# Text tokens' inner products in four 32-column tiles of TensorE, from each block's diagonal on

## The chip, the cores and the metric

One core of one Trainium2 chip. The metric is the time of one execution on the device in microseconds. Three runs of the kernel before took 433.48, 433.68 and 434.69 us; the median is 433.68 us.

## The reference, cut to what matters

Cross attention with 8 batches, 112 queries of 320 channels, 20 heads of 16 channels, and a context of 375 tokens of 512 channels, of which the last 4 are prompt tokens and the first 371 text tokens.

```python
q, k_t, v_t = heads(x @ W_q), heads(text @ W_k), heads(text @ W_v)
probs_t  = softmax(q . k_t * 16**-0.5)              # 112 x 371 for each batch and head
text_out = probs_t @ v_t
qsem     = l2norm(probs_t @ text)                   # 112 x 512 for each batch and head
sem      = qsem @ l2norm(ip).T                      # against the 4 prompt tokens
probs_ip = softmax(q . k_ip * scale + 0.5 * sem) * spatial_mask
out      = (text_out + probs_ip @ v_ip) @ W_out + b_out + x
```

The norm of `probs_t @ text` is the square root of p^T G p, where G = text text^T are the text tokens' inner products (371 x 371, symmetric). The kernel therefore never forms `qsem`: it computes G once for each batch, and from G the norms of all 20 heads.

## The kernel before

Each batch goes through 5 groups of 4 heads; a group is a step, and there are 40 steps.

*The Gram matrix.* `gram(b)` computes G in three chunks c0, c1, c2 of 128 token rows, each in a PSUM bank of its own named `ps_g`. A chunk's matmuls take 128 tokens of the transposed context as the stationary operand and the tokens from the chunk's start to the end, prompts included, as the moving one: 375, 247 and 119 columns, over four channel blocks `e`. Each float32 matmul is two hardware passes, so a Gram is 24 loads of weights and 24 passes. Only the upper triangle by chunks is made; `doubled` evicts a chunk with one ScalarE instruction that multiplies by 2 (line 443) and then has GpSimd multiply the diagonal chunk by the mask `half` (line 444), which halves the 32 x 32 blocks on the diagonal, so that the half triangle stands for the whole G. `ug` is the SBUF tile that receives this; one buffer serves all batches. Batch 0's Gram is made by `first_gram` in another order, and calls `doubled` too.

*From the Gram to the products.* `gram_to_groups` copies `ug` by DMA, four DMAs for each block of 32 partitions, to the tile `u` of the batch, where every 32-partition group holds the same tokens for another head. The values (line 526, evicted at line 533 to `vext`) are written to DRAM by `values_to_dram`, read back by `values_to_groups` into `vr` and put behind the Gram's columns in `u` by `placed` on GpSimd. `product` (line 683) multiplies the transposed probabilities of one head, 32 tokens at a time, with the matching 32 rows of `u`, from the diagonal on: 12 products j for each head, 392 columns wide for j = 0 and 32 narrower each time, 40 for the last. The four heads of a group lie on the four 32-row groups of TensorE and write to four banks.

*The order.* The instructions of TensorE, VectorE and SyncE stand in the order in which they are written, and after a prologue those of ScalarE and GpSimd as well. `pair(n)` writes the products of two steps, with the scores (line 632) and probabilities (lines 645 to 658) of the steps two ahead between them; where it passes from one step to the next it writes

```python
for there, here in ((HIGH, LOW), (LOW, HIGH)):
    product(*two, 0, there)
    for j in ends:
        product(b, g, j, here)
```

`behind(n)` writes the projections of the coming batches behind each pair: queries, keys, Gram (`gr`), values, and pieces of the last batch's `finish` (`f`). For an odd batch the three chunks of the Gram are written with other pieces between them, the third behind a piece of `finish` whose ScalarE work is a square root with a table load on either side (lines 801 and 802):

```python
gr(nb); tr(0); gr(nb)
if n: f(b - 1)
gr(nb)
...
v(nb)
```

For an even batch (`gr(nb + 1, 3)`) all three follow each other. Batch 1's Gram is followed by the projections of the prompts (lines 271 and 288), for which GpSimd spreads the weights `wip` (lines 123 and 124).

*The banks.* PSUM has four banks with the tag "qd" and two each with "sc" and "mm"; each tag hands its banks out in turn. `turn` says which tag the next projections take. For odd batches c0, c1 and c2 take three "qd" banks and the values' first chunk an "mm" bank; for even batches c0 takes "qd" and c1 and c2 take "mm". The four products of the next step take the four "qd" banks, and a product waits until its bank has been evicted. Two of the coming scores take "mm" banks.

Of the kernel before, what the change touches and what calls it, by code (L numbers as in the profile page):

```python
# [8 lines left out]
F32 = mybir.dt.float32  # L9
AF = mybir.ActivationFunctionType  # L10
ALU = mybir.AluOpType
# [9 lines left out]
def kernel(  # L21
# [29 lines left out]
    RG = 32  # L51
# [11 lines left out]
    QN = P // RG  # L63
    WC = [UW - c * P for c in range(NT)]
    GCOL = [sum(WC[:c]) for c in range(NT + 1)]
    GW = GCOL[NT]
    UCOL = QN * GW
    assert (H, D, NC, NT, P) == (20, 16, 3, 3, 128) and RG == 2 * D


    groups = [[i * HC + 2 * a + r for a in range(GROUP)] for i in range(2) for r in range(2)]
    groups.append([2 * HC + a for a in range(GROUP)])

    const = ctx.enter_context(tc.tile_pool(name="const", bufs=1))
# [94 lines left out]
    make_identity(nc, ident)  # L169
    nc.gpsimd.memset(wq_sb[REST:, FULL, :], 0.0)  # L170

    half = const.tile([P, P], F32, tag="half", name="half")
    nc.gpsimd.memset(half, 1.0)
    for q in range(QN):
        nc.gpsimd.memset(half[q * RG : (q + 1) * RG, q * RG : (q + 1) * RG], 0.5)

    hmask = const.tile([P, HC], F32, tag="hmask", name="hmask")
    nc.vector.tensor_reduce(
# [10 lines left out]
    ug = const.tile([P, GCOL[NT]], F32, tag="ug", name="ug")  # L189
# [17 lines left out]
    k3 = const.tile([P, NT, GROUP, 2, D], F32, tag="k3", name="k3")  # L207

    def more_constants():
        nc.gpsimd.memset(k3[:, :, :, 1, :], 0.0)  # L210
        nc.gpsimd.memset(wo_sb[REST:, FULL, :], 0.0)
        for at in attn_ring:
            nc.gpsimd.memset(at[:, C:], 0.0)
# [130 lines left out]
    st = {}  # L344
# [93 lines left out]
    def doubled(ps, c):  # L438

        t0 = c * P  # L440
        k = min(P, TT - t0)
        g = ug[:, GCOL[c] : GCOL[c] + T - t0]
        nc.scalar.mul(g, ps[:, : T - t0], 2.0)  # L443
        nc.gpsimd.tensor_tensor(g[:, :k], g[:, :k], half[:, :k], ALU.mult)  # L444

    def gram(b):

        ctxT = st[b]["ctxT"]

        for c in range(NT):  # L450
            t0 = c * P
            ps = bank(f"ps_g_{b}_{c}")
            for e in range(NE):
                nc.tensor.matmul(  # L454
                    ps[:, : T - t0],
                    ctxT[:, e, t0 : t0 + P],
                    ctxT[:, e, t0:T],
                    start=(e == 0),
                    stop=(e == NE - 1),
                )  # L460
            doubled(ps, c)
            yield

    def gram_to_groups(b, blocks):
# [74 lines left out]
            yield  # L539

    def values_to_dram(b, eng, c0=0, c1=NT):
        eng.dma_start(
            st[b]["vd"][c0 * P : c1 * P].rearrange("(c p) x -> p c x", p=P),
            st[b]["vext"][:, c0:c1, :C],
        )

    def values_to_groups(b):
        s = st[b]
# [128 lines left out]
    def product(b, g, j, heads):  # L677
        s = st[b]
        xT = s["xT", g]
        banks = s["qd", g]  # L680
        c, q = j // QN, j % QN
        for a in heads:
            nc.tensor.matmul(  # L683
                banks[a][:S, j * RG : UW],
                xT[a * RG : (a + 1) * RG, j, :S],
                region(b, c)[a * RG : (a + 1) * RG, q, q * RG :],
                start=(j == 0),
                stop=(j == BLK - 1),
            )
# [395 lines left out]
    def gr(b, pieces=1):  # L1085
        run(("g", b), lambda: gram(b), pieces)
# [192 lines left out]
    for n in range(0, len(steps) - NG, 2):  # L1279
# [4 lines left out]
        b, g = steps[n]  # L1284
# [16 lines left out]
    b = B - 1  # L1301
# [12 lines left out]
    for g in range(NG):  # L1314
# [20 lines left out]
        if g < NG - 1:  # L1335

            n = GROUP - 1 if g <= LEAD else 1
# [89 lines left out]
```

## Time and profile before

| | us |
|---|---|
| median of three runs | 433.68 |
| the profiled execution | 434.62 |
| its span, first to last instruction | 432.9 |
| PE busy | 423.2 (98%) |
| DVE busy | 328.5 (76%) |
| ACT busy | 190.7 (44%) |
| POOL busy | 112.1 (26%) |

PE stands for TensorE's matmuls, PEld for its weight loads, DVE for VectorE, ACT for ScalarE, POOL for GpSimd, SP for SyncE, whose queue issues most DMAs. A group's row gives the line, the engine, the operation, the tiles it writes and reads, the shape and the count; then the busy time in us, the mean duration of one in ns, and the idle time of the engine just before, with what ended it. A shape such as 32*112 is rows by columns of the stationary operand. A timeline row gives the start in us, the length in us of a merged run of instructions, and their count. The granted clock of TensorE was 0.995 of full speed over the span.

### The profile page before, as it was taken

How to read it: one execution, taken by the hardware profiler on the slowest of the kernel's cores; microseconds unless marked ns; L12 is line 12 of the kernel's file. 1: busy time of each engine (PE TensorE's matmuls, PEld its weight loads, DVE VectorE, ACT ScalarE, POOL GpSimd, SP SyncE). 2: the span in 40 equal slices, each digit the busy share in tenths (PEclk: the TensorE clock that was granted, in tenths of full speed). 3: DMA queues.
4: the chain of work that ended last, by engine and by line, in shares of the span. 5: the costliest groups of instructions: out<-in, count | busy, mean ns of one | idle time of the engine just before them, and what ended most of it. 6: DMA issues, size and time to landing. Idle time of an engine off the chain costs nothing. (4 is left out here: it accounts for less than half of the span.)

```text
span 432.9 us, 12985 instructions
## 1 busy us (share of the span) xinstructions
PE 423.2 (98%) x5024; PEld 323.8 (75%) x5024; DVE 328.5 (76%) x687; ACT 190.7 (44%) x649; POOL 112.1 (26%) x270
## 2 busy tenths in 40 slices
PE   8999999999999999999999999999999999999986
PEld 8756677778686887778686887778776888776783
DVE  4045467797899897796889898787888897778884
ACT  2264123334553454333643464233633563346793
POOL 4302200012151234012142126002133226026440
PEclk9999899999999999999999999999999999999999
DMA  8669946487554566576744466575755436663300
GB/s 243 171 173 248 213 112 154 143 192 155 148 142 123 157 160 150 152 177 138 181 134 124 127 171 159 144 187 134 173 160 145 111 101 166 175 157 100 101 4 27
DMA packets 57931, 64.21 MB, mean 148 GB/s; under 512 B 18368, under 2 KB 52024, under 8 KB 57870
## 3 DMA queue, kind: packets, MB, share of 16 engines
q1 hardware_dynamic: 57304, 62.66, 57.2%
q8 instruction: 40, 0.66, 0.7%
q10 hardware_dynamic: 566, 0.72, 0.5%
q14 instruction: 21, 0.17, 0.1%
HBM read 18.67 MB, written 5.32 MB: 55 GB/s over the span
## 5 line engine op out<-in xcount | busy, mean ns | idle before, releaser
L683 PE MATMUL ps_qd<-u,xgT 32*112 32x232 f32 (+11 forms) x3840 | 215.4, 352 | 1.9 <-POOL u L599 1.9
L683 PEld LDWEIGHTS ps_qd<-u,xgT 32*112 32x112 f32 x3840 | 180.0, 172 | 36.5 <-issue 8.1
L672 DVE STREAM_TRANSPOSE xgT<-xg 128x768 f32<-128x768 f32 (+1 forms) x63 | 121.2, 1951 | 9.2 <-DMA xg<-p 9.1
L649 ACT ACTIVATE p<-ps_s,nmx 112x371 f32<-112x371 f32 x160 | 85.8, 586 | 52.5 <-DVE nmx L645 48.5
L743 DVE CUSTOM_DVE_ANT_0 junk<-ps_qd,p 112x371 f32<-112x371 f32 x148 | 80.2, 542 | 31.5 <-ACT pvs L710 11.4
L645 DVE TENSOR_REDUCE nmx<-ps_s 112x1 f32<-112x371 f32 x160 | 77.3, 537 | 28.0 <-PE ps_s L632 26.0
L599 POOL COPY u<-vr 128x64 f32<-128x64 f32 x120 | 26.7, 237 | 192.9 <-PE ps_qd L683 116.4
L526 PE MATMUL ps_v<-wv_sb,ctxT 128*128 128x384 f32 (+1 forms) x192 | 63.5, 477 | 0.3 <-ACT kT L499 0.3
L632 PE MATMUL ps_s<-kT,qm 32*112 32x375 f32 (+1 forms) x320 | 61.9, 487 | 1.0 <-ACT shared L728 0.7
L526 PEld LDWEIGHTS ps_v<-wv_sb,ctxT 128*128 128x128 f32 x192 | 35.4, 190 | 20.7 <-ACT kT L499 1.2
L710 ACT COPY pvs<-ps_qd 112x21 f32<-112x21 f32 x150 | 21.4, 200 | 62.2 <-DVE ss L743 61.0
L492 PE MATMUL ps_k<-ctxT,wk_sb 128*128 128x371 f32 x136 | 45.8, 481 | 0.0
L454 PE MATMUL ps_g<-ctxT 128*128 128x375 f32 (+2 forms) x168 | 36.8, 375 | 0.0
L454 PEld LDWEIGHTS ps_g<-ctxT 128*128 128x128 f32 x168 | 28.3, 191 | 8.7
L492 PEld LDWEIGHTS ps_k<-ctxT,wk_sb 128*128 128x128 f32 x136 | 24.6, 190 | 13.4 <-issue 0.5
L632 PEld LDWEIGHTS ps_s<-kT,qm 32*112 32x112 f32 x320 | 27.9, 171 | 6.9 <-ACT shared L728 1.3
L533 ACT COPY vext<-ps_v 128x384 f32<-128x384 f32 (+1 forms) x24 | 11.2, 466 | 37.1 <-PE ps_v L526 37.0
L651 ACT COPY ipl<-ps_s 112x4 f32<-112x4 f32 x140 | 24.2, 173 | 0.0
L443 ACT ACTIVATE ug<-ps_g 128x375 f32<-128x375 f32 (+2 forms) x24 | 9.0, 377 | 29.4 <-PE ps_g L454 20.5
L499 ACT COPY kT<-ps_k 128x371 f32<-128x371 f32 x17 | 8.0, 469 | 30.8 <-PE ps_k L492 30.8
L336 DVE TENSOR_SCALAR qm<-ps_q,emask 128x224 f32<-128x224 f32 (+1 forms) x25 | 8.9, 395 | 15.9 <-PE ps_q L327 15.9
L444 POOL TENSOR_TENSOR ug<-ug,half 128x128 f32<-128x128 f32 (+1 forms) x24 | 10.8, 448 | 35.3 <-ACT ug L443 35.0
(160 smaller groups left out, 333.5 us busy)
## 6 DMA issues: line engine op xcount, KB each, us to landing
xg<-p SPq DMA_DIRECT2D x159, 162.3 KB
u<-ug SPq DMA_DIRECT2D x128, 99.0 KB
ct<-in_ctx_dram SPq DMA_DIRECT2D x24, 176.0 KB
vr<-vd SPq DMA_DIRECT2D x32, 120.0 KB
vip<-vipd SPq DMA_DIRECT2D x6, 560.0 KB
vd<-vext SPq DMA_DIRECT2D x4, 480.0 KB
out_dram<-ob SPq DMA_DIRECT2D x8, 140.0 KB
ct<-in_ctx_dram SPq DMA_DIRECT2D x4, 256.0 KB
```

Of the source, the lines that this page charges most:

```text
L454: nc.tensor.matmul(ps[:, : T - t0], ctxT[:, e, t0 : t0 + P], ctxT[:, e, t0:T], start=(e == 0), stop=(e == NE - 1),)
L492: nc.tensor.matmul(ps[:, :TT], wk_sb[:, e, i * P : (i + 1) * P], s["ctxT"][:, e, :TT], start=(e == 0), stop=(e == NE - 1),)
L526: nc.tensor.matmul(ps[:, :w], ctxT[:, e, c * P : (c + 1) * P], wv_sb[:, e, :w], start=(e == 0), stop=(e == NE - 1),)
L599: nc.gpsimd.tensor_copy(region(b, c)[:, :, UV - c * P :], s["vr"][:, c * QN : (c + 1) * QN, g, :])
L632: nc.tensor.matmul(ps[:S, :w], qm[a * RG : (a + 1) * RG, i, r, j * S : (j + 1) * S], s["kT"][a * RG : (a + 1) * RG, i, :w], start=True, st ...
L645: nc.vector.tensor_reduce(nmx, ps[:S, :TT], AX.X, ALU.max, negate=True)
L649: nc.scalar.activation(p, ps[:S, :TT], AF.Exp, bias=nmx)
L651: nc.scalar.copy(s["ipl"][:, groups[g][a], :], ps[:S, TT:T])
L672: nc.vector.transpose(xT[:, j : j + n].rearrange("p j (k q) -> p q j k", q=QN), xg[:, :, j * RG : (j + n) * RG].rearrange("p q (j k) -> p ...
L683: nc.tensor.matmul(banks[a][:S, j * RG : UW], xT[a * RG : (a + 1) * RG, j, :S], region(b, c)[a * RG : (a + 1) * RG, q, q * RG :], start=(j ...
L710: nc.scalar.copy(s["pvs"][:, h, :], ps[:S, TT:UW])
L743: nc.vector.tensor_tensor_reduce(out=junk, in0=ps[:S, :TT], in1=s["p", g][:, a, :], scale=1.0, scalar=0.0, op0=ALU.mult, op1=ALU.add, accu ...
```

## The change

For batches 1 to 7 every matmul of a Gram chunk is split into four with 32 stationary columns each, one for each block q of 32 tokens in the chunk. Each writes to another 32 partitions of the bank and so uses another group of 32 columns of the array (a column tile). The moving operand of block q starts at its own diagonal, so it is 32 q columns shorter. Which block goes to which tile differs from chunk to chunk (`DEAL`), so that each tile gets wide and narrow blocks. The eviction of a chunk becomes four ScalarE instructions of 32 partitions, each from its diagonal on; GpSimd's masking stays one instruction, with a mask of its own for each chunk. Since the blocks of `ug` now lie in another order, `product` looks up the place of its block, and the values are written to DRAM in the same order, with one DMA for each run of neighbouring blocks: one for c0, three for c1 and two for c2. Batch 0 keeps its order and its instructions.

```diff
+    DEAL = ((0, 1, 2, 3), (2, 3, 1, 0), (3, 0, 1, 2))
+
+    def dealt(b, c):
+        return DEAL[c] if b > 0 else DEAL[0]
...
+    half = const.tile([P, NT, P], F32, tag="half", name="half")
+    def halves(c):
+        nc.gpsimd.memset(half[:, c, :], 1.0)
+        for p, q in enumerate(DEAL[c]):
+            nc.gpsimd.memset(half[p * RG : (p + 1) * RG, c, q * RG : (q + 1) * RG], 0.5)
+    halves(0)
...
     def more_constants():
+        for c in range(1, NT):
+            halves(c)
...
             for e in range(NE):
-                nc.tensor.matmul(
-                    ps[:, : T - t0],
-                    ctxT[:, e, t0 : t0 + P],
-                    ctxT[:, e, t0:T],
-                    start=(e == 0),
-                    stop=(e == NE - 1),
-                )
-            doubled(ps, c)
+                for p, q in enumerate(DEAL[c]):
+                    nc.tensor.matmul(
+                        ps[p * RG : (p + 1) * RG, q * RG : T - t0],
+                        ctxT[:, e, t0 + q * RG : t0 + (q + 1) * RG],
+                        ctxT[:, e, t0 + q * RG : T],
+                        start=(e == 0),
+                        stop=(e == NE - 1),
+                    )
+            k = min(P, TT - t0)
+            g = ug[:, GCOL[c] : GCOL[c] + T - t0]
+            for p, q in enumerate(DEAL[c]):
+                here = slice(p * RG, (p + 1) * RG)
+                nc.scalar.mul(g[here, q * RG :], ps[here, q * RG : T - t0], 2.0)
+            nc.gpsimd.tensor_tensor(g[:, :k], g[:, :k], half[:, c, :k], ALU.mult)
             yield
...
     def values_to_dram(b, eng, c0=0, c1=NT):
...
+        for c in range(c0, c1):
+            q = 0
+            while q < QN:
+                p, n = DEAL[c].index(q), 1
+                while q + n < QN and p + n < QN and DEAL[c][p + n] == q + n:
+                    n += 1
+                to = c * P + p * RG
+                eng.dma_start(
+                    s["vd"][to : to + n * RG], s["vext"][q * RG : (q + n) * RG, c, :C]
+                )
+                q += n
...
+        p = dealt(b, c).index(q)
...
-                region(b, c)[a * RG : (a + 1) * RG, q, q * RG :],
+                region(b, c)[a * RG : (a + 1) * RG, p, q * RG :],
```

More of the change, by code (lines that the diff above doesn't have):

```diff
@@ L170 @@
     nc.gpsimd.memset(wq_sb[REST:, FULL, :], 0.0)
[L172 to L175, printed above, removed]
+    half = const.tile([P, NT, P], F32, tag="half", name="half")
[4 more added lines that the diff above has]
+    halves(0)
     hmask = const.tile([P, HC], F32, tag="hmask", name="hmask")
@@ L443, in doubled @@
         nc.scalar.mul(g, ps[:, : T - t0], 2.0)
-        nc.gpsimd.tensor_tensor(g[:, :k], g[:, :k], half[:, :k], ALU.mult)
+        nc.gpsimd.tensor_tensor(g[:, :k], g[:, :k], half[:, 0, :k], ALU.mult)
     def gram(b):
@@ L541, in values_to_dram @@
     def values_to_dram(b, eng, c0=0, c1=NT):
[L542 to L545, printed above, removed]
+        s = st[b]
+        if b == 0:
+            eng.dma_start(
+                s["vd"][c0 * P : c1 * P].rearrange("(c p) x -> p c x", p=P),
+                s["vext"][:, c0:c1, :C],
+            )
+            return
+        for c in range(c0, c1):
[5 more added lines that the diff above has]
+                to = c * P + p * RG
+                eng.dma_start(
+                    s["vd"][to : to + n * RG], s["vext"][q * RG : (q + n) * RG, c, :C]
+                )
+                q += n
     def values_to_groups(b):
```

## The prediction

> **What bounds the kernel now.** I read the head of the page first, then the stretches of two text Gram matrices (windows), then the timelines of PE, ACT, DVE and POOL around three of them. "Gram" is the kernel's `ps_g`, its chunks are c0, c1, c2.
>
> ```profile
> span 432.9 us, 12985 instructions
> PE 423.2 (98%) x5024; PEld 323.8 (75%) x5024; DVE 328.5 (76%) x687; ACT 190.7 (44%) x649; POOL 112.1 (26%) x270
> ```
>
> PE sets the time: 98% busy, so a microsecond taken from PE counts if nothing else is late in its place, and a wait put in front of PE counts in full. The Gram's share, for batches 3 and 4 (columns: stretch, its length, PE busy and count, weight loads, clock, DMA):
>
> ```profile
> 146.32:151.40 5.08, 5.08 (x24) 3.91 (x24) 1.00 0.69 194
> 191.09:196.16 5.07, 5.07 (x24) 3.90 (x23) 1.00 0.85 178
> ```
>
> Each batch's Gram is one unbroken stretch of 5.08 us on PE: four channel blocks, two hardware passes each, of 375, 247 and 119 columns, which is 8 x 741 = 5928 columns at 0.857 ns. All seven together are 35.6 us, the most that is at stake.
>
> **Part 1, the matmuls.** A pass becomes four of 32 stationary columns, in four column tiles. Over c0, c1, c2 the tiles stream 375+183+23, 343+151+119, 311+215+87 and 279+247+55 columns, so 581, 613, 613, 581. The trace of before has no four column tiles at work, so I bound their joint speed by its row tiles, where four 32-row products share the array. Whether such tiles advance on their own shows where `pair` hands over: the program writes the next group's 392-wide products of two heads before the 72- and 40-wide products of the other two. Groups by shape in the window 139.9 to 140.45 us:
>
> ```profile
> L683 PE MATMUL ps_qd<-u,xgT 32*112 32x392 f32 x2 | 0.5, 497 | 0.0
> ...
> L683 PE MATMUL ps_qd<-u,xgT 32*112 32x104 f32 x8 | 0.4, 252 | 0.0
> L683 PE MATMUL ps_qd<-u,xgT 32*112 32x72 f32 x4 | 0.3, 244 | 0.0
> L683 PE MATMUL ps_qd<-u,xgT 32*112 32x40 f32 x4 | 0.3, 247 | 0.0
> ```
>
> The two narrow products of two heads have run both passes (x4, x4) while the wide ones, written earlier, have started only the first (x2). Row tiles advance independently. If column tiles do too, a Gram costs its widest tile, 8 x 613 x 0.857 = 4.20 us, 0.88 less. If they start in the order written, tile 0's next pass waits for its last and the others follow: 375, then 247, then 119 columns a round, 5.08 as before. I take independence, as the nearest row shows it.
>
> The Trainium skill says otherwise, in "TensorE: Matmul & The Clock Gate", Part 3, "The mechanism": tiled matmuls start and end in strict program order. For row tiles the rows above contradict it; for column tiles no row here decides. By it the sum would be that of the first rival.
>
> A change of tiling is added in front of each Gram (the one behind exists). PE and by-shape rows around batch 4's and batch 3's Gram:
>
> ```profile
> 191.09 5.23 PE L454 MATMUL ps_g<-ctxT 128*128 128x375 f32 x24
> 196.26 1.22 PE L683 MATMUL ps_qd<-u,xgT 32*112 32x392 f32 x10
> ```
>
> ```profile
> L683 PE MATMUL ps_qd<-u,xgT 32*112 32x392 f32 x3 | 0.6, 578 | 0.0
> ```
>
> The stretch ends at 196.16, the first product starts at 196.26: 0.10; and a first 392-wide pass behind such a change takes 578 ns where 497 stood above: 0.08 to 0.09. I take 0.19 us a Gram. So PE gains 0.88 - 0.19 = 0.69 us (or loses 0.19 in lockstep).
>
> **Part 2, the evictions.** Three ACT instructions become twelve, of 32 partitions and the tile's width.
>
> ```profile
> L443 ACT ACTIVATE ug<-ps_g 128x375 f32<-128x375 f32 x8 | 3.9, 483 | 18.1 <-PE ps_g L454 10.2 <-DMA ct<-in_ctx_dram 3.7 <-PE ps_g L427 2.1
> ...
> L443 ACT ACTIVATE ug<-ps_g 128x247 f32<-128x247 f32 x8 | 3.0, 377 | 8.7 <-PE ps_g L454 8.3 <-PE ps_g L427 0.4
> ```
>
> ```profile
> 41.70 0.41 ACT L710 COPY pvs<-ps_qd 112x21 f32<-112x21 f32 x4 [1.26 <-PE ps_qd L683]
> ```
>
> 483 and 377 for 375 and 247 columns give 0.83 ns a column and about 0.17 us fixed. Back to back the fixed part overlaps: four 21-column copies in 0.41 us follow each other by about 0.07, of which 0.017 is columns, so each occupies ACT 0.05 us plus its columns. Fewer partitions don't shorten it. c0: 0.20 + 0.83 ns x 1308 = 1.29 us instead of 0.36; c1: 0.20 + 0.66 = 0.87 instead of 0.26; c2: 0.20 + 0.24 = 0.44 instead of 0.15. That is 1.8 us more ACT a batch. At 44% ACT could carry it; the question is who stands behind.
>
> *Odd batches 3, 5, 7.* ACT, then PE, around batch 3's Gram, then PE by shape up to 154.30 us:
>
> ```profile
> 149.05 0.48 ACT L443 ACTIVATE ug<-ps_g 128x375 f32<-128x375 f32 x1 [1.36 <-PE ps_g L454]
> 150.71 0.38 ACT L443 ACTIVATE ug<-ps_g 128x247 f32<-128x247 f32 x1 [1.18 <-PE ps_g L454]
> 151.11 1.28 ACT L801 ACT_TABLE_LOAD   x1
> 152.40 0.22 ACT L801 ACTIVATE rn<-rn 112x20 f32<-112x20 f32 x1
> 152.64 1.28 ACT L802 ACT_TABLE_LOAD   x1
> 153.93 0.27 ACT L443 ACTIVATE ug<-ps_g 128x119 f32<-128x119 f32 x1
> 154.23 0.48 ACT L533 COPY vext<-ps_v 128x384 f32<-128x384 f32 x1
> ```
>
> ```profile
> 146.32 5.24 PE L454 MATMUL ps_g<-ctxT 128*128 128x375 f32 x24
> 151.40 2.75 PE L526 MATMUL ps_v<-wv_sb,ctxT 128*128 128x384 f32 x8
> 154.08 1.22 PE L683 MATMUL ps_qd<-u,xgT 32*112 32x392 f32 x10
> ```
>
> ```profile
> L683 PE MATMUL ps_qd<-u,xgT 32*112 32x392 f32 x4 | 0.8, 578 | 0.0
> ```
>
> The square root of the batch before, with a table load on either side, stands in ACT's queue between c1's and c2's eviction. The product of head 3 takes c2's bank (the four "qd" banks are handed out in turn): only three first products have started by 154.24 (the x3 row above), the fourth by 154.30, behind the eviction that ends at 153.93 + 0.27 = 154.20. So here PE already waits for ACT. After the change: c0 starts 0.19 later, at 149.24, and leaves ACT at 150.53; c1's last slice (247 columns) starts 0.61 later, at 151.14, and the table load 0.40 behind it as now: 151.54, which is 0.43 late. c2 begins at 154.36, its last slice 0.34 later and 0.22 long: 154.92, head 3 at 154.97 instead of 154.26. PE finishes Gram and values 0.69 us earlier and then waits: **+0.72 us each, +2.15 for three**; heads 0 to 2 run one step ahead but cannot finish without head 3.
>
> *Even batches 2, 4, 6.* PE, ACT and DVE rows around batch 4's (PE's stand above):
>
> ```profile
> 193.86 0.48 ACT L443 ACTIVATE ug<-ps_g 128x375 f32<-128x375 f32 x1 [3.71 <-DMA ct<-in_ctx_dram]
> 195.54 0.38 ACT L443 ACTIVATE ug<-ps_g 128x247 f32<-128x247 f32 x1 [1.20 <-PE ps_g L454]
> 196.43 0.27 ACT L443 ACTIVATE ug<-ps_g 128x119 f32<-128x119 f32 x1 [0.51 <-PE ps_g L454]
> ```
>
> ```profile
> 190.96 4.37 DVE L672 STREAM_TRANSPOSE xgT<-xg 128x1536 f32<-128x1536 f32 x2
> ```
>
> No table load here. c0's bank is free at 193.86 + 0.19 + 1.29 + about 0.13 = 195.47, the products would start at 196.26 - 0.69 = 195.57, and DVE's transposes are over at 195.33: all three just fit. **-0.69 each, -2.07 for three**, at best; with c0's bank or DVE a little late, -0.4 each.
>
> *Batch 1.* POOL and PE:
>
> ```profile
> 47.40 0.43 POOL L444 TENSOR_TENSOR ug<-ug,half 128x115 f32<-128x115 f32 x1 [0.32 <-ACT ug L443]
> 47.77 0.71 POOL L123 COPY wip<-wip 128x64 f32<-128x64 f32 x3
> 48.54 0.31 POOL L124 MEMSET wip<- 128x256 f32 x1
> ```
>
> ```profile
> 48.90 1.08 PE L271 MATMUL ps_kip<-ipT,wip 128*128 128x32 f32 x8 [0.23 <-POOL wip L124]
> ```
>
> PE waits for POOL, whose spread of the prompt weights stands behind the last masking. With c2 evicted at about the old time, 0 to +0.1; an earlier Gram ends in the same wait. Batch 0 is untouched.
>
> **Part 3, DMAs and POOL.** The values' DRAM write becomes six DMAs for an odd batch (one, three and two by chunk), four and two for an even one. SP rows:
>
> ```profile
> 175.36 0.40 SPq L542 DMA_DIRECT2D vd<-vext  x1
> 177.56 3.65 SPq L658 DMA_DIRECT2D xg<-p  x4
> ```
>
> Five more at about 0.40 + 0.05 are 2.25 us against 1.80 us of idle SP before the next probabilities, so those leave up to 0.45 late in odd batches; their transposes are needed a group later. I book +0.2 each, 0.6 in all (from 0 to 1.4). Even batches stay in the idle time. Ten more memsets at the start lie in idle POOL time. The products themselves keep their shapes.
>
> **Sum.** 2.15 - 2.07 + 0.05 + 0.6 = +0.7 us. The profiled execution was 434.62 us (span 432.9 and 1.7 around it), 0.94 above the median of 433.68 and within the runs' spread; a difference goes on the median: **434.4 us**, no change by the 0.3% (1.3 us) that a measurement of this kernel can tell.
>
> **Rivals.**
> *Lockstep.* Column tiles start in the order written. Even batches then pay the change of tiling (3 x 0.19 = 0.6); in odd ones c1 comes to ACT at 150.90, the load at 150.90 + 0.61 + 0.40 = 151.91, head 3 at 155.34: 1.08 each, 3.25; batch 1's last masking is 0.45 later and PE with it; 0.6 for SP. +4.9 us, **438.6**. It decides as soon as tile 3 cannot run ahead of tile 0 in c0. For it: the tiles share all 128 rows, which the row tiles of this trace don't. Against it: the independent row tiles. It is the case of the Trainium skill's rule weighed in part 1.
> *One after another.* Loads or passes of different column tiles don't overlap. Their sum is 8 x 2388 columns x 0.857 = 16.4 us a Gram, 11.3 more, **513** for all seven. If only the loads queue, the nearest row is a load of 32 columns:
>
> ```profile
> L288 PEld LDWEIGHTS ps_vip<-wip,ipT 128*32 128x32 f32 x8 | 1.2, 168 | 2.2 <-issue 2.1
> ```
>
> 96 a Gram at 0.1 to 0.17 us (mostly at a lowered clock there) are 9.6 to 16 us, so 465 and more. Against it: full-array loads run beside matmuls in the windows above (3.91 us of loads in a gapless 5.08). The same section of the Trainium skill's page has loads overlap running matmuls only where the row groups differ, which speaks against this change; those full-array rows, where the row groups are the same, don't agree with it.
> *ACT's bill is smaller.* If small slices overlap further on ACT, or head 3's lag is made up behind, odd batches cost nothing and even ones gain: 433.7 - 2.07 = **431.6**; the floor, all seven gaining 0.69, is 428.9. Against it: the x3 and x4 rows, where PE stands at ACT's mercy already.
>
> **How the numbers follow.** Forecast 0.48, lockstep 0.28, one after another 0.10, the smaller bill 0.14. Of the forecast's own spread (even batches -0.4 to -0.69, SP 0 to 1.4, so +0.1 to +2.4) I give a quarter to slower by over 1.3 us and a tenth to faster. Faster: 0.05 + 0.13 = 0.18; same: 0.31 less a little, 0.29; slower: 0.12 + 0.28 + 0.10 and that little, 0.53. The range leaves out the serial case and the lower half of the smaller bill: 431.8 to 440.0.
>
> **What would show it.** Right: a Gram stretch of about 4.2 us on PE with tile 3 ahead of tile 0; twelve evictions of 1.29, 0.87 and 0.44 us; in odd batches PE's idle time ended by ACT `ug` after a table load, 0.7 us later than now in Gram time; none in even ones. Wrong: a Gram of 5 us or more (lockstep), over 9 us (one after another), or products of head 3 that start without waiting for c2.

## The result and the profile after

The kernel after takes **452.99 us** (median of 4 executions, 449.38 to 453.69), the kernel before 433.86 us (433.48 to 434.69) beside it: a ratio of **1.042**, 95% interval 1.037 to 1.046. The forecast was 434.4 us, its range ended at 440.0. Medians and ranges below are of all executions of a kernel; the ratios leave out those at a disturbed clock.

The profiled execution took 449.38 us, the least of the four, and its granted clock was 0.992 of full speed where the three others had 0.985 to 0.988: 2 to 3 us more for them, an estimate from 0.004 to 0.007 of 450 us. So the traces below explain the 14.8 us of this execution, not the whole 19.1 between the medians. The head of its page, with the groups of the changed lines:

```profile
span 447.7 us, 14137 instructions
...
PE 428.2 (96%) x5528; PEld 332.1 (74%) x5528; DVE 330.4 (74%) x687; ACT 210.6 (47%) x712; POOL 113.4 (25%) x280
...
L715 PE MATMUL ps_qd<-u,xgT 32*112 32x104 f32 (+11 forms) x3840 | 222.3, 355 | 9.8 <-ACT ug L477 5.2
...
L477 ACT ACTIVATE ug<-ps_g 32x375 f32<-32x375 f32 (+5 forms) x84 | 27.5, 327 | 18.6 <-PE ps_g L466 16.9
L663 PEld LDWEIGHTS ps_s<-kT,qm 32*112 32x112 f32 x320 | 29.0, 173 | 8.0 <-ACT ug L477 1.8
...
L466 PE MATMUL ps_g<-ctxT 128*32 128x375 f32 (+11 forms) x672 | 32.1, 335 | 0.0
```

PE went from 98% to 96% of a longer span. The Gram's own line, L466, lost nothing to waiting (0.0 idle). The products, L715, now stand idle for `ug`, which ACT writes at L477: 84 instructions, 27.5 us. The list of PE's waits (engine, what waits, on whom: us in total, times, longest) says where:

```profile
PE ps_qd L715 <- ACT ug L477: 5.2, 3, 2.0
PE ps_qd L715 <- POOL u L630: 4.1, 3, 2.3
PE ps_kip L282 <- POOL wip L129: 2.1, 1, 2.1
```

Three waits for ACT, one in each odd batch; three for the block `u`, of which one of 2.3 us stands before batch 6; and batch 1's wait for POOL's spread, 2.1 us. Before, the same list has no wait of PE for `ug`; `u` 1.9 in two, `wip` 0.2.

The timeline of ACT around batch 3's Gram (start, length, group), which answers to the rows from 149.05 on in the prediction:

```profile
152.08 3.20 ACT L477 ACTIVATE ug<-ps_g 32x375 f32<-32x375 f32 x8 [1.52 <-PE ps_g L466]
155.30 1.28 ACT L833 ACT_TABLE_LOAD   x1
156.59 0.22 ACT L833 ACTIVATE rn<-rn 112x20 f32<-112x20 f32 x1
156.83 1.28 ACT L834 ACT_TABLE_LOAD   x1
158.13 0.94 ACT L477 ACTIVATE ug<-ps_g 32x23 f32<-32x23 f32 x4
159.09 0.48 ACT L550 COPY vext<-ps_v 128x384 f32<-128x384 f32 x1
```

And of PE:

```profile
149.29 4.59 PE L466 MATMUL ps_g<-ctxT 128*32 128x375 f32 x96
153.80 2.85 PE L543 MATMUL ps_v<-wv_sb,ctxT 128*128 128x384 f32 x8
156.58 0.92 PE L715 MATMUL ps_qd<-u,xgT 32*112 32x392 f32 x6
159.12 0.58 PE L715 MATMUL ps_qd<-u,xgT 32*112 32x392 f32 x1 [1.62 <-ACT ug L477]
```

PE is through with the Gram in 4.59 us (5.24 before). The evictions of c0 and c1 take 3.20 us without a break, so the table load starts at 155.30, 1.42 us behind the Gram's end (149.29 + 4.59), where before it started 0.45 us ahead of it. c2's bank comes free at 159.07, and the product of head 3 starts at 159.12 after 1.62 us in which PE has nothing else to do.

**Where the 14.8 us of span went.** I set the starts of the first product of every step in the two profiled executions side by side; the differences add up to 14.8 us:

| where | us |
|---|---|
| start-up, ahead of the first changed Gram | +0.8 |
| batch 1, PE behind POOL's spread | +1.25 |
| batches 2, 4, 6: -0.44 to -0.55, then +1.05 to +1.16 | +1.9 |
| batches 3 and 5: -0.14 to -0.38, then +2.12 and +0.24 | +4.2 |
| batch 7: -0.24, then +4.00 | +3.8 |
| before batch 6: +0.49 and the wait for `u`, +2.43 | +2.9 |

Start-up differs by -0.7 to +1.1 us between the kernels of this study, also where nothing there was changed. Near 50 us, behind batch 1's Gram, the clock is at half for 3.4 us in both executions. Batch 7 has the same wait for ACT as batches 3 and 5 and something more, which the windows around it show (stretch, its length, PE and weight loads busy, DVE, ACT, POOL, granted clock, DMA):

```profile
361.00:365.60 4.60, 2.60 (x16) 1.20 (x18) 3.65 (x8) 4.47 (x11) 1.57 (x3) 1.00 0.03 8
365.60:369.05 3.45, 3.45 (x29) 2.94 (x25) 1.15 (x3) 1.42 (x6) 0.07 (x1) 0.51 0.01 2
369.05:372.00 2.95, 2.95 (x69) 2.93 (x65) 2.79 (x6) 1.14 (x4) 0.24 (x2) 1.00 0.50 135
```

PE waits until 365.22, and from 365.6 to 369.05 its clock is at half. Batch 7's two losses come to 4.00 us where those of batches 3 and 5 come to 2.12 + 0.24, so the stretch cost about 1.6 us.

### The profile page after: what moved, and what is told of

It reads as the page before. It is cut to its first block, busy times and chain, and to the rows that moved or that the text cites. A ratio compares the mean times of both kernels' runs of the same rounds, so it can differ in the third digit from the quotient of the medians.

```text
span 447.7 us, 14137 instructions
## 1 busy us (share of the span) xinstructions
PE 428.2 (96%) x5528; PEld 332.1 (74%) x5528; DVE 330.4 (74%) x687; ACT 210.6 (47%) x712; POOL 113.4 (25%) x280
## 5 line engine op out<-in xcount | busy, mean ns | idle before, releaser
L715 PE MATMUL ps_qd<-u,xgT 32*112 32x104 f32 (+11 forms) x3840 | 222.3, 355 | 9.8 <-ACT ug L477 5.2
L715 PEld LDWEIGHTS ps_qd<-u,xgT 32*112 32x112 f32 x3840 | 187.9, 172 | 42.5 <-issue 8.9
L703 DVE STREAM_TRANSPOSE xgT<-xg 128x768 f32<-128x768 f32 (+1 forms) x63 | 122.6, 1972 | 10.3 <-DMA xg<-p 9.8
L663 PE MATMUL ps_s<-kT,qm 32*112 32x375 f32 (+1 forms) x320 | 66.6, 497 | 1.1 <-ACT shared L760 0.7
L477 ACT ACTIVATE ug<-ps_g 32x375 f32<-32x375 f32 (+5 forms) x84 | 27.5, 327 | 18.6 <-PE ps_g L466 16.9
L663 PEld LDWEIGHTS ps_s<-kT,qm 32*112 32x112 f32 x320 | 29.0, 173 | 8.0 <-ACT ug L477 1.8
L466 PE MATMUL ps_g<-ctxT 128*32 128x375 f32 (+11 forms) x672 | 32.1, 335 | 0.0
L466 PEld LDWEIGHTS ps_g<-ctxT 128*32 128x32 f32 x672 | 26.9, 109 | 5.4 <-POOL u L630 1.0
L478 POOL TENSOR_TENSOR ug<-ug,half 128x128 f32<-128x128 f32 (+1 forms) x21 | 9.6, 455 | 46.3 <-ACT ug L477 46.3
```

The lines of the kernel that those rows point to most:

```text
L466: nc.tensor.matmul(ps[p * RG : (p + 1) * RG, q * RG : T - t0], ctxT[:, e, t0 + q * RG : t0 + (q + 1) * RG], ctxT[:, e, t0 + q * RG : T], s ...
L477: nc.scalar.mul(g[here, q * RG :], ps[here, q * RG : T - t0], 2.0)
L663: nc.tensor.matmul(ps[:S, :w], qm[a * RG : (a + 1) * RG, i, r, j * S : (j + 1) * S], s["kT"][a * RG : (a + 1) * RG, i, :w], start=True, st ...
L703: nc.vector.transpose(xT[:, j : j + n].rearrange("p j (k q) -> p q j k", q=QN), xg[:, :, j * RG : (j + n) * RG].rearrange("p q (j k) -> p ...
L715: nc.tensor.matmul(banks[a][:S, j * RG : UW], xT[a * RG : (a + 1) * RG, j, :S], region(b, c)[a * RG : (a + 1) * RG, p, q * RG :], start=(j ...
```

## The experiments

**One part alone: the evictions in slices.** The kernel before, its own matmuls, no deal, no added DMAs.

```diff
-            doubled(ps, c)
...
+            for q in range(QN):
+                here = slice(q * RG, (q + 1) * RG)
+                nc.scalar.mul(g[here, q * RG :], ps[here, q * RG : T - t0], 2.0)
+            nc.gpsimd.tensor_tensor(g[:, :k], g[:, :k], half[:, :k], ALU.mult)
```

> The kernel before with one part of the change: every Gram chunk of batches 1 to 7 is evicted by four ScalarE multiplications of 32 partitions, each from its diagonal on; matmuls, order of blocks and DMAs stay. Theory 'evictions' (the twelve multiplications of a batch run one behind the other, 4.2 us instead of 1.1, and PE waits for the banks): in odd batches head 3's product about 1.9 us late each, in even ones the scores about 0.5 us, batch 1 about 1 us, so +7 to +12 us, 441 to 446 us. Rival 'tiles' (column tiling itself slows PE or its clock): within 1 us of before. Rival 'DMAs' (the split writes of the values): within 1 us of before.

Measured: 447.08 us (444.15 to 449.85), ratio 1.030 (1.022 to 1.037), a little over the 441 to 446 expected. Step by step: batch 1 +1.3, even batches +0.45 each, odd ones +1.6 to 1.8 and 0.24 behind. PE's waits in it:

```profile
PE ps_qd L688 <- ACT ug L465: 3.7, 3, 1.5
PE ps_qd L688 <- POOL u L604: 1.8, 2, 1.0
PE ps_kip L271 <- POOL wip L124: 1.6, 1, 1.6
```

Sliced evictions alone, with nothing else of the change, bring most of the loss and the same waits for `ug` and `wip`. They don't bring all of it: behind the start-up the steps lose 9.1 us here and 14.0 in the kernel after. Of the 4.9 us between them 2.1 lie before batch 6 and some 1.7 in the half-clock stretch of batch 7.

**The rest of the change without them.** The kernel after with one eviction of 128 partitions a chunk; so that the whole bank is written, the first channel block's passes have full width, the other three start at the diagonal.

```diff
+                    d = q * RG if e else 0
...
-                        ps[p * RG : (p + 1) * RG, q * RG : T - t0],
+                        ps[p * RG : (p + 1) * RG, d : T - t0],
-                        ctxT[:, e, t0 + q * RG : T],
+                        ctxT[:, e, t0 + d : T],
...
-            for p, q in enumerate(DEAL[c]):
-                here = slice(p * RG, (p + 1) * RG)
-                nc.scalar.mul(g[here, q * RG :], ps[here, q * RG : T - t0], 2.0)
+            nc.scalar.mul(g, ps[:, : T - t0], 2.0)
```

> The kernel after with one eviction of 128 partitions a chunk, as before the change; for this the passes of the first channel block stream the chunk's whole width, the other three start at the diagonal; dealing and DMAs stay. 'Evictions': PE gains about 0.6 us a Gram in even batches, odd ones and batch 1 about nothing; 432 to 436 us, the upper end if the DMAs cost. 'Tiles': the loss stays, 445 us and more. 'DMAs': some 436 to 440 us.

Measured: 435.48 us (432.33 to 441.24), ratio 1.001 (0.997 to 1.004). The loss of 4% is gone with the slices, and PE waits for `ug` no more. Up to batch 7 the profiled execution is 2.1 us ahead of before, from 1.0 behind at its start. But 2.3 of these 3.1 us come at batch 1, where the kernel before has a half-clock stretch (49.95 to 53.36 us) and this execution has none; all later Grams bring 0.8. It ends 1.0 us later all the same. The windows show why (columns as above, clock third from the end):

```profile
420.80:427.60 6.80, 6.80 (x17) 3.89 (x17) 2.96 (x16) 2.87 (x7) 0.00 (x0) 0.50 0.00 0
```

Its clock is at half for 6.8 us of the tail. Its two executions at a clock of 0.999 and more took 432.33 and 432.94.

**Column tiles alone.** All passes at full width in four tiles, no deal, one eviction, one DMA for the values; the edit is against the kernel after.

```diff
-    DEAL = ((0, 1, 2, 3), (2, 3, 1, 0), (3, 0, 1, 2))
+    DEAL = ((0, 1, 2, 3),) * 3
...
+                    d = 0
...
-                        ps[p * RG : (p + 1) * RG, q * RG : T - t0],
+                        ps[p * RG : (p + 1) * RG, d : T - t0],
...
-                        ctxT[:, e, t0 + q * RG : T],
+                        ctxT[:, e, t0 + d : T],
...
-                nc.scalar.mul(g[here, q * RG :], ps[here, q * RG : T - t0], 2.0)
+            nc.scalar.mul(g, ps[:, : T - t0], 2.0)
...
-        if b == 0:
+        if True:
```

> Column tiles alone: every pass in four column tiles of the whole width, blocks in their own order, one eviction a chunk, the values written as before. 'Evictions' and 'DMAs': Gram 5.1 to 5.3 us on PE, 434 to 435 us. 'Tiles': 445 us and more, or a granted clock clearly under 0.995.

Measured: 435.66 us (434.07 to 438.85), ratio 1.003 (1.000 to 1.005), a little over the 434 to 435 expected. Four tiles of 741 columns take as long as one array of 741 (96 passes in 5.21 us, the 24 of before 5.23), so the extra loads of 32 columns cost nothing that shows, and the change of tiling little: the ratio is 1.1 us for seven Grams with an interval of 0 to 2.3, and the steps lose 0.07 us in an even batch and 0.15 in an odd one.

**Copies instead of multiplications.** The kernel after; the factor 2 goes into the scale of the scores.

```diff
-SEM_SCALE = 0.5
+SEM_SCALE = 0.5 * 2.0**0.5
...
-                nc.scalar.mul(g[here, q * RG :], ps[here, q * RG : T - t0], 2.0)
+                nc.scalar.copy(g[here, q * RG :], ps[here, q * RG : T - t0])
```

> The kernel after with the twelve evictions as plain copies in place of multiplications by 2; the factor is taken into the constant SEM_SCALE, so the output is the same. If it is the multiplication that does not overlap with its successor: c0 in 1.3, c1 in 0.9, c2 in 0.45 us of ScalarE, 435 to 439 us. If instructions on different partitions never overlap: evictions as in the kernel after, 4.2 us together, 449 us and more. 'Tiles': no change from after.

Measured: 451.03 us (449.37 to 452.18), ratio 1.037 (1.033 to 1.041). Copies, which follow each other by 0.07 us in the row that the prediction rests on, don't overlap here either. Ten of batch 4's twelve slices in its timeline:

```profile
199.55 3.60 ACT L477 COPY ug<-ps_g 32x375 f32<-32x375 f32 x10 [3.88 <-PE ps_g L466]
```

Ten take 3.60 us, as in the kernel after. The instruction's kind isn't the cause. What then keeps slices apart, when copies of 21 columns overlap?

**As many instructions of all partitions.** The kernel before, each chunk multiplied out four times, in the slices' widths, by 128 partitions; then the same with the three extra ones on partitions 0 to 31.

```diff
...
+            for q in range(1, QN):
+                nc.scalar.mul(g[:P, q * RG :], ps[:P, q * RG : T - t0], 2.0)
             doubled(ps, c)
```

> The kernel before, but in batches one to seven each Gram chunk is multiplied out of its bank four times, by instructions of all 128 partitions and of the four tile widths (343, 311, 279 and last 375 columns for chunk 0, and so on), so there are as many ACT instructions and columns as in the kernel after, without its 32-partition slices. Theory 'place' (ACT overlaps back-to-back instructions on the same partitions, and not those on other partitions): they follow each other about 0.05 us faster than they last plus 24 ns, that is every 0.83 ns a column and 0.05 us, so about 1.3, 0.9 and 0.45 us a batch of chunks and about 435.5 to 439 us in all (odd batches +0.7, even +0.6, batch one +0.5). Theory 'count' (twelve instructions in a row never overlap here, whatever their partitions): 1.8, 1.4 and 0.95 us, as in the kernel with four 32-partition slices and the old matmuls, and 445 to 449 us.

> As the run with four evictions of 128 partitions, but the three extra ones take the first 32 partitions alone, each time the same ones, and the last takes all 128. Theory 'place': they overlap, about 0.83 ns a column and 0.05 us from one to the next, and the time is 435.5 to 439 us. Theory 'few partitions' (instructions of 32 partitions don't overlap, wherever they lie): each lasts in full with 24 ns between, chunk 0 takes 1.8 us, and the time is 445 to 449 us.

Measured: 448.56 us (445.01 to 449.66, ratio 1.030, 1.026 to 1.034) and 448.49 us (one execution). By the letter both theories of place fall. But the test was spoilt by its make: each of the four writes elements that the one ahead of it wrote, and the program as built puts a wait of ACT on its own semaphore between them. A chunk's instructions follow each other 32 ns after the last one's end, not 24 as in most slices. Where no such wait stands, from the full eviction of c0 to c1's first piece in the second kernel, they overlap:

```profile
199.51 0.48 ACT L443 ACTIVATE ug<-ps_g 128x375 f32<-128x375 f32 x1
199.89 0.98 ACT L463 ACTIVATE ug<-ps_g 32x215 f32<-32x215 f32 x3
```

c1's piece starts 0.38 us after an instruction of 0.48. So these two kernels show what three more long instructions a chunk cost when they can't overlap, and nothing on why slices can't.

**Pieces that share no element.** In even batches four column pieces of 128 partitions, in odd ones four column pieces of partitions 0 to 31 and then partitions 32 to 63 and 64 to 127 whole.

```diff
-            doubled(ps, c)
...
+            cuts = [(T - t0) * i // QN for i in range(QN + 1)]
+            first = P if b % 2 == 0 else RG
+            for x0, x1 in zip(cuts, cuts[1:]):
+                nc.scalar.mul(g[:first, x0:x1], ps[:first, x0:x1], 2.0)
+            for part in (slice(RG, 2 * RG), slice(2 * RG, P)):
+                if first < P:
+                    nc.scalar.mul(g[part], ps[part, : T - t0], 2.0)
```

> The kernel before, but each Gram chunk of batches one to seven is multiplied out of its bank in pieces that overlap in no element: in even batches four column pieces of all 128 partitions (c0: 93 or 94 columns each), in odd ones four such pieces of partitions 0 to 31, then partitions 32 to 63 and 64 to 127 at full width. Theory 'place' (ACT starts an instruction before the last has ended only if both begin at the same partition): the column pieces follow each other every 0.12 to 0.14 us though each lasts some 0.25, in even and odd batches alike, and the 32-to-63 piece starts only after the piece before it has ended, 24 ns later. Theory 'few partitions' (32-partition instructions never overlap): the column pieces overlap in even batches only, and follow each other every 0.27 us in odd ones. Theory 'same bank' (instructions that read one bank never overlap): every 0.27 us in both. The time: 435 to 437 us by the first, up to 441 by the others.

Measured: 444.70 us (one execution). That is 8 us over the 435 to 437 of the first theory, and over the 441 of the others too. The odd batches lost it: their last two pieces of a chunk run at full length, and a step loses 1.4 to 1.6 us in each, batch 1 1.2. The even batches, with column pieces alone, lose 0.0 us in their steps, where slices cost 0.45. The rows of ACT's timeline say what was asked. Batch 4, then batch 3, and for batch 3 the groups by shape (busy, mean ns):

```profile
197.00 0.67 ACT L466 ACTIVATE ug<-ps_g 128x93 f32<-128x93 f32 x4 [3.72 <-PE ps_g L454]
...
150.57 0.63 ACT L466 ACTIVATE ug<-ps_g 32x93 f32<-32x93 f32 x4 [1.36 <-PE ps_g L454]
151.23 0.98 ACT L469 ACTIVATE ug<-ps_g 32x375 f32<-32x375 f32 x2
152.24 0.52 ACT L466 ACTIVATE ug<-ps_g 32x61 f32<-32x61 f32 x4
152.77 0.75 ACT L469 ACTIVATE ug<-ps_g 32x247 f32<-32x247 f32 x2
```

```profile
L466 ACT ACTIVATE ug<-ps_g 32x94 f32<-32x94 f32 x3 | 0.5, 226 | 0.0
...
L469 ACT ACTIVATE ug<-ps_g 64x247 f32<-64x247 f32 x1 | 0.4, 372 | 0.0
L469 ACT ACTIVATE ug<-ps_g 32x247 f32<-32x247 f32 x1 | 0.4, 369 | 0.0
```

Four pieces of some 0.23 to 0.25 us each are over in 0.63 us on 32 partitions, and in 0.67 on 128: they start every 0.13 us, so few partitions don't hinder, nor does one bank. But 32 to 63 behind 0 to 31, and 64 to 127 behind that, take 0.75 us for 0.369 + 0.372, with nothing in the program to wait for: no overlap. Nor is a wait needed to keep slices apart in the kernel after: pairs there that neither wait nor signal start 11 to 12 ns after the end of the one ahead. On this evidence ACT runs instructions into each other only where both begin at the same partition. That is how the slices of the change differ from every row on which the prediction relied. Two pieces that both begin at partition 32, or at any other than 0, were not tried.

**The table loads out of the way.** The kernel after, in odd batches with the square root behind c2.

```diff
             gr(nb)
+            gr(nb)
             if n:
                 f(b - 1)
-            gr(nb)
```

> The kernel after, but in odd batches the piece of the batch before with the square root and its two table loads (2.8 us of ACT) is written behind the third Gram chunk instead of ahead of it. Theory 'evictions': the stall of head 3 behind chunk 2's eviction (2.0 to 2.1 us in each of three odd batches) shrinks to what the even batches lose, about 0.6 us each, so 4 to 5 us less than the kernel after: about 447 to 449 us, with PE's waits for ug down from 5.2 us to under 1.5. Rival 'the eviction of chunk 0 is late by itself, the table load only follows': under 1.5 us less, 450.5 us or more.

Measured: 448.07 us (444.47 to 449.54), ratio 1.030 (1.026 to 1.034), about 5 us under the kernel after, as the first theory had it. PE's list of waits has no `ug` any more, but a new entry:

```profile
PE ps_qd L715 <- POOL u L630: 3.8, 3, 1.6
PE ps_s L663 <- ACT vext L550: 2.9, 3, 1.1
```

The table loads now stand ahead of the values' copy, and the next scores want its bank. An odd batch still loses about 1.1 us net where it lost 2.0 to 2.2. The table loads made the stall longer; its cause is ACT's 4.17 us of slices where three evictions took 0.48 + 0.38 + 0.27.

**The DMAs alone.** The kernel before with the values written in one, three and two DMAs.

```diff
...
+        RUNS = (((0, 4),), ((0, 1), (1, 1), (2, 2)), ((0, 3), (3, 1)))
+        for c in range(c0, c1):
+            for q, n in RUNS[c]:
+                to = c * P + q * RG
+                eng.dma_start(
+                    s["vd"][to : to + n * RG], s["vext"][q * RG : (q + n) * RG, c, :C]
+                )
```

> The kernel before, with the values of batches one to seven written to DRAM in one, three and two DMAs by chunk as the kernel after does, and nothing else changed. Theory 'DMAs count': SP issues 0.3 to 0.6 us for each, the reads of batch 6's values start late by 2 us or more, PE waits for POOL's u, and the time is 1.5 to 3 us above before. Theory 'evictions' (the late values of batch 6 came from everything before them being late): 0 to 0.6 us above before.

Measured: 435.61 us (434.81 to 440.81), ratio 1.003 (1.001 to 1.006), that is 0.4 to 2.5 us, and +1.0 us in the steps of the profiled execution behind its start-up. This lies between the two theories. Before batch 6 the steps lose only 0.24 us, so in the kernel before there is just room for the DMAs.

**Fewer evictions and one DMA for the values.** Four more runs ask whether the tiles' gain can be had. First one eviction a chunk with the square root behind c2 (the two edits above together):

> The kernel after with one 128-partition eviction a chunk, and with the square-root piece of the batch before behind the third Gram chunk in odd batches. Theory 'the evictions ate the gain': even batches keep 0.2 to 0.4 us, odd ones now also 0.3 to 0.5 (head 3 no longer waits for the table loads), less about 0.8 for the six DMAs of the values: 431.5 to 434.5 us against 434.8 before. Rival 'the tables only move': PE then waits for ACT's copy of the values behind the table loads, 1 us in each odd batch, and the time is 436 us or more.

Measured: 436.44 us (431.52 to 439.65), ratio 1.000 (0.997 to 1.003). Executions at a clock of 0.999 and more took 431.52 to 433.40, those at 0.995 and less 435.99 and up. The median is in the rival's range, but the rival's mechanism isn't there: PE has no wait for ACT's copy of the values. In the profiled execution, the slowest of the twelve, PE waited 2.2 us for `u` before batch 6, and a stretch at half clock followed. Then the values in one DMA in token order, in the kernel after and in this one:

```diff
-        if b == 0:
+        if True:
             eng.dma_start(
```

> The kernel after, but the values of batches one to seven are written to DRAM in one DMA, in token order (so the products of the text values belong to the wrong rows in these batches; shapes, counts and all other work are as after). Theory 'late and then DMAs' (in the kernel after, batch 6 waited 2.4 us for its values because SP carries five more issues in a stage that the evictions had already made late): the wait before batch 6 goes from 2.4 to under 0.5 us and the time is 448 to 450.5 us. Rival 'evictions alone': the wait stays, and the time is within 1 us of the kernel after (450.5 us or more).

> The kernel with one 128-partition eviction a chunk and the square root behind the third chunk, and the values of batches one to seven written to DRAM in one DMA, in token order (so the products of the text values belong to the wrong rows in these batches; shapes, counts and all other work stay). It bounds what column tiles could bring if the dealt order cost no DMAs. Theory 'DMAs make batch 6 late, and the pause is followed by half-clock stretches': no wait of over 0.5 us before batch 6, and most executions at 430.5 to 433 us, a median 2 us or more below before. Rival 'the half-clock stretches come anyway': the executions spread over 431 to 438 us as with six DMAs, median within 1 us of before.

Measured: 451.14 us (449.44 to 451.52), ratio 1.036 (1.033 to 1.040), and **432.81 us** (430.53 to 435.25), ratio **0.995** (0.993 to 0.998). In both the wait before batch 6 is gone. In the first the time hardly moved, and neither theory has both the wait and the time right: a stretch at half clock, behind batch 5's wait for ACT this time, took 1.7 us, and the stretch near 50 us was twice as long as in the kernel after, with 1.6 us more lost at batch 1. In the second the steps gain 2.1 us behind batch 1, and the median lies 1.9 below before; six of its twelve executions were within the 430.5 to 433 expected of most. The reads of batch 6's values in the rows of SP, for the kernel after, the one with six DMAs and a single eviction, and the one with one DMA, each from its own timeline:

```profile
343.17 1.85 SPq L582 DMA_DIRECT2D vr<-vd  x4
```

```profile
332.14 1.85 SPq L581 DMA_DIRECT2D vr<-vd  x4
```

```profile
329.45 1.87 SPq L581 DMA_DIRECT2D vr<-vd  x4
```

The pair that begins with batch 5's last group started on PE at 341.69, 330.96 and 330.33 in them: the reads come 1.5 us behind that, 1.2 us behind, and 0.9 us ahead, and batch 6's first products lose 2.4, 2.35 and 0 us. SP falls behind PE by its added issues, but they are not enough for so long a wait: with the same six DMAs the reads come 0.3 us behind in the kernel before and 0.2 behind in the run with one eviction and the square root in its old place, and 0.2 us is lost in each. Why moving the square root makes them later was not taken apart.

At last the values made in the dealt order by column tiles of their own, which need one DMA and leave nothing in the wrong order:

```diff
-    DEAL = ((0, 1, 2, 3), (2, 3, 1, 0), (3, 0, 1, 2))
+    DEAL = ((0, 1, 2, 3), (3, 2, 1, 0), (0, 1, 2, 3))
...
-                    ps[:, :w],
-                    ctxT[:, e, c * P : (c + 1) * P],
...
+                        ps[p * RG : p * RG + n, :w],
+                        ctxT[:, e, c * P + q * RG : c * P + q * RG + n],
...
-                        ident[:rows, :rows],
+                        (redeal if c == 1 else ident)[:rows, :rows],
```

> The kernel with one 128-partition eviction a chunk and the square root behind the third chunk, and with the values made in the dealt order by column tiles of their own (32 tokens stationary each, 384 or 320 columns), so that one DMA writes them; the deal is 0123, 3210, 0123 (widest tile 645 columns instead of 613), and the transposed keys of the second chunk are put back by a permuted identity. Theory 'DMAs make batch 6 late': the gain of the run with one DMA in token order stays, less 0.2 us a Gram for the wider tile: 431.5 to 434 us, no wait of over 0.5 us before batch 6. Rival 'a pass in four tiles costs more than one of 128 columns': the values, 24 passes of 384 columns a batch in the kernel before, take 0.3 us or more longer a batch, and the time is 435 us or more.

Measured: 434.56 us (432.60 to 438.42), ratio 1.001 (0.998 to 1.004), between the ranges of the two theories. No wait before batch 6, but behind batch 1 it gives back 0.8 us of its lead where the run with one DMA in token order gained 2.1: some 0.5 us a batch, of which the wider tile is 0.2. The values' passes themselves are not the rest: batch 3's take 8.51 us in three places where they took 8.44. It may lie with the changes of tiling around them; that was not taken apart further. No kernel that computes everything in its right order beat the kernel before.

## Why the prediction was wrong

**The matmuls: right in kind, the gain 0.56 to 0.65 us a Gram instead of 0.88.** Column tiles run ahead of one another. From its first pass to the pass behind it the Gram takes 4.52 us where it took 5.08 (odd batches) to 5.16 (even ones), and 4.20 were forecast. The passes of tile 3 of c0 run ahead of tile 0's; in the kernel after, 1.7 us behind the start of batch 3's Gram (window 149.25 to 151.0 us), tile 3 (279 columns) has started all its eight passes of c0 and tile 0 (375 columns) six:

```profile
L466 PE MATMUL ps_g<-ctxT 128*32 128x375 f32 x6 | 2.1, 482 | 0.0
L466 PE MATMUL ps_g<-ctxT 128*32 128x279 f32 x8 | 2.1, 401 | 0.0
```

But they are not wholly free of each other, which the sum took them to be. From 152.14 us on tile 1's passes of 151 columns, which had followed each other every 0.13 us, come every 0.15, each 4 to 6 ns behind a pass of tile 0 that stands two passes earlier in its own order. Tile 1 is one of the two widest: at its undisturbed pace of 0.288, 0.128 and 0.101 us a pass its 24 passes would take an estimated 4.14 us, and they took 4.42. That is most of what is missing from the forecast; what sets this limit the runs don't show. Even batches reach their first product 0.44 to 0.55 us earlier, odd ones 0.14 to 0.38 (0.69 forecast at best); the change of tiling, put at 0.19 us a Gram, cost 0.07 to 0.15 in the run with column tiles alone. Both rivals on PE fall: lockstep wanted a Gram of 5 us, one after another over 9. The rule of the Trainium skill ("TensorE: Matmul & The Clock Gate", Part 3, "The mechanism") that tiled matmuls start and end in program order doesn't agree with these rows. The sentence of the same section of the Trainium skill that loads overlap running matmuls only where the row groups differ doesn't either: 672 loads of 32 columns cost nothing that the run with column tiles alone could show.

**The step that failed: "Back to back the fixed part overlaps".** The twelve evictions of a batch were put at 1.29, 0.87 and 0.44 us. They measured 1.81, 1.37 and 0.94: each takes its full length and 11 to 24 ns more. The row behind the step, four copies of 21 columns in 0.41 us, is of 112 partitions from the same first one; the slices start at 0, 32, 64 and 96. The prediction's own sentence "Fewer partitions don't shorten it" was right (375 columns take 472 ns on 32 partitions, 483 on 128), and the one that needed a row, whether instructions of *different* partitions overlap, had none in the trace. It should have been bounded from both sides: without overlap 0.17 us and 0.83 ns a column for each slice, 1.8 us for c0 and 4.0 for the batch, from the same two rows; that bound was close to what came, and belonged in the sum and the range. In the profiled execution the wrong bill shows as +8.0 us in the odd batches (2.15 forecast; some 1.6 of it is the half-clock stretch), +1.9 in the even ones (-2.07 forecast) and +1.25 in batch 1 (0.05 forecast).

**Odd batches.** The mechanism was right, head 3 behind c2's eviction behind the table load: forecast +0.72 each, measured +2.2 and +2.0 in batches 3 and 5. From the Gram's start on, the load comes 1.22 us later than before (6.01 against 4.79 us; 0.43 forecast), as c0 and c1 fill 3.2 us without a break where 2.2 us of work were forecast; c2's own 0.94 instead of 0.27 us adds 0.67. Together 1.89, which is what head 3 shows: 9.83 us behind the Gram's start instead of 7.94.

**Even batches.** Forecast -0.69 and no wait; the gain of about 0.5 came, and then +1.1 which I had not seen: scores take the banks of c1 and c2 next (L663, loads idle 1.8 us for `ug`), and those are free only 3.2 and 4.2 us after c0's eviction began. That "all three just fit" was worked out for c0's bank alone.

**Batch 1 and the DMAs.** Batch 1 was booked at 0 to +0.1 and cost 1.25: POOL's masking, and with it the spread of the prompt weights, stands behind c2's last slice, which was taken to be on time. The DMAs were booked at 0.6, bound 1.4; alone they cost 0.4 to 2.5. In the kernel after, where the evictions have already made the values later, they also bring a loss of 2.4 us before batch 6, which is gone with one DMA; the prediction had only probabilities leaving late in odd batches.

**The rival of ACT's smaller bill** (431.6) went the wrong way: the bill was larger. No rival had it larger. The run without slices and with one DMA, 432.81, comes near that rival's figure, but by having no slices, not by cheap ones; so some of the gain on PE was there to be had, at the price of the wrong order of the values.

## What to carry to other kernels

Before splitting an eviction by partitions, look for a row in which the engine runs instructions of *different* first partitions one after the other, and without one cost each piece at its full length. Splitting matmuls into column tiles cost 0 to 2.3 us for seven Grams here, taking their results away in slices 10 to 16 (ratio 1.022 to 1.037). Cost it for every bank of the group and for whoever takes that bank next, not for the first alone. And where SP issues transfers in order, count its lead over PE in the stage: the reads of batch 6's values were 0.7 us ahead in the kernel before, and with six DMAs for these values where two stood they came 0.3 us behind.

## What the runs showed of the hardware

- ACT starts the next instruction before the last one has ended where both begin at the same partition: pieces of 94 columns and 0.22 to 0.27 us every 0.13 us, on 32 partitions as on 128. With another first partition it waits for the end: 369 + 372 ns took 0.75 us. The pieces that overlapped all begin at partition 0; others were not tried.
- Passes of four column tiles overtake one another: eight of 279 columns had started when six of 375 had. A Gram whose widest tile streams 613 columns a block took 4.52 us, that of 741 columns in four equal tiles 5.14, to the next pass.
- PE's clock falls to half for 3.4 us or twice that, in nearly every kernel here near 50 us, and in the tail of many. Whether the first of these is there changes a comparison of two profiled executions: batch 1 came out 2.3 to 2.5 us earlier than before in the two that had none. In the middle it was seen five times (in the kernel after at 365.6, and in four experiments), each time within 1.5 us of the end of a wait of PE of 1.5 to 2.2 us; most such waits were not followed by one. Where one followed, the loss was 1.5 to 1.7 us more than the wait. That the wait brings the stretch on is a guess from these five; why some are followed and some not stays open.
- The kernels with less work on PE spread more: with one eviction a chunk and the square root moved 431.5 and 439.7 us came out of the same kernel, and lower granted clocks went with the longer times, where the kernel before stayed within 433.3 and 437.6. With one DMA in the same kernel the spread fell to 430.5 to 435.3, so late values may have a part in it; but with the values in dealt order, and no wait for them, it was 432.6 to 438.4 again, and the cause stays open.
